# A four-layer mixture-of-experts kernel: the capacity search gets buffers of its own, normalised rows come from ScalarE, and layer 3's gate and up run as two float32r passes

## The chip, the cores and the metric

The kernel runs on one core of a Trainium2 chip. The metric is the device time of one execution in microseconds (us), the median of several runs. Lower is better. The engines are named as the profile names them: PE (TensorE matmuls), PEld (its weight loads), DVE (VectorE), ACT (ScalarE), POOL (GpSimd) and SP (SyncE, which issues most DMAs).

## What is computed

An input of 16 sequences of 256 tokens with 128 features (4096 tokens) goes through four layers. Each layer normalises its input and adds two branches to it:

```python
xn = layernorm(x)
x = x + attn_l(xn) + ffn_l(xn)
```

- Layer 0: attention with 16 heads of 8 features and rotary angles; a mixture of 8 experts (128 to 512 to 128, ReLU), two per token. Each expert keeps at most 1280 tokens, those with the largest gates: a gate under its expert's 1280th largest becomes zero.
- Layer 1: a linear recurrence over each sequence with two projections and a normalisation; 15 experts (128 to 128 to 128), three per token, and one shared expert.
- Layer 2: attention without a bias; 8 experts (128 to 512 to 128), one per token.
- Layer 3: causal attention with a position-dependent bias and an output projection; a dense gated branch, whose weights are integers from -127 to 127, scaled by 1/127:

```python
gate, up = xn @ wg.T, xn @ wu.T        # 128 to 384, wg = w_gate / 127
ffn = (silu(gate) * up) @ wd.T         # 384 to 128
```

## The kernel before

**Tiles.** Tokens stand on the 128 partitions. A block is 512 tokens, so there are 8 blocks; `xb[i]` holds a block of x in SBUF throughout. Routed experts work on groups of blocks: two groups of 4 blocks in layers 0 and 2, four groups of 2 blocks in layer 1 (`GRP`, line 34).

**Order.** Every engine runs its instructions in the order in which they are written, and that order is not written by hand. The code records every operation (class `Engine`, line 312; all of them carry line 350 in the profile), and `Plan.order` (line 186) makes a list for each engine from assumed costs, dependences, free buffers and a due time for each stage and group (`WANTED`, lines 37 to 59). `COLD` (line 35) scales the assumed PE cost. Two score operations on different 32-row strips of the array may be woven together, so that they run at once.

**Buffers.** A tile belongs to a ring, named by its tag, with so many buffers. Within one stream of work (the second argument of `plan.run`) tiles of a ring are taken in turn: as long as a task that has begun still has tiles of the ring to take, no other task of the stream takes one.

**The steps that matter here.**

- `normalize` (line 552): statistics and an inverse root for each token on DVE (`moments`, `inverse_root`), then four DVE operations per block that make `xn`. Four PE transposes and an ACT copy give `xT`. This is done 32 times, for 8 blocks in 4 layers.
- `route_0` (line 1090): router logits of a group, softmax and top two. The gates go to `g0`, which holds all 4096 tokens, expert by expert.
- `sort` (line 1214): gives every choice a place in a table of rows ordered by expert. It takes a tile `m` from the ring `cap` (three buffers) and, in `ranks` (line 673), one from the ring `rank` (one buffer). It ends with indirect DMAs on POOL (line 710), 32 for a group in layer 0, that scatter the rows of `xn`.
- `capacity` (line 627): finds the 1280th largest gate of each expert, bit by bit. Each of 30 steps compares all gates with a candidate (`cap_cmp`), counts (`part_b`), sums over the partitions by a small matmul (`tot_b`) and keeps or drops the bit (`hit`, `cap_thr`). It takes tiles of `cap` and `rank` as well, and it runs in the stream `sort`, emitted after the two sorts of layer 0. Only the combination of layer 0 needs its result.
- `some_tiles` and `slots` (lines 1274 and 727): for every 128 sorted rows an expert's weights are fetched (ring `we`, four buffers) and two matmuls done (`ph`, `po`). The results are gathered by indirect DMA on POOL and added to x in `combine` (line 775).
- Attention: `queries_keys` (line 815) makes queries and keys (`pq`), splits each into a rounded part and a remainder (`half`; in layer 0 with two POOL additions `rope` and `half`), and spreads and fetches them through DRAM (`qm`, `km`, `qx`, `kx`). `front` takes the row maxima of the scores on DVE (`mraw`), `back` the exponentials on ACT (`e`) and the value products (`av`).
- `ffn_3` (line 1325): gate and up are float32 matmuls on `xT` (`pp`, 128 by 512), then tanh on ACT, two DVE products and the down matmul (`po`). `weights_3` (line 1312) loads the three integer matrices as one tile and scales them.

Of the kernel before, what the change touches and what calls it, by code (L numbers as in the profile page):

```python
# [28 lines left out]
BT = 4  # L29
# [4 lines left out]
GRP = {0: 4, 1: 2, 2: 4, 3: 2}  # L34
COLD = 1.2
# [3 lines left out]
    "": (62.9, 0.0, 0.0, 0.0),  # L39
    "att0": (-17.7, 39.8, 36.9, 120.1),  # L40
    "att2": (-125.2, 4.9, -67.1, 45.9),
    "att3": (-85.1, 46.0, 51.1, 102.8),
    "bias2": (-56.2, 153.4, 126.8, 401.9),
    "f3": (166.9, 61.0, 85.4, -51.3),
    "ffn0": (-34.4, 0.0, 32.5, 0.0),
    "ffn1": (2.9, 54.3, 149.0, 145.3),
    "ffn2": (-212.1, 0.0, -158.9, 0.0),
    "kept": (-12.8, 0.0, 0.0, 0.0),
    "rec": (31.1, 105.4, 174.5, 249.2),
    "route0": (-57.1, 0.0, -13.2, 0.0),  # L50
    "route1": (-194.8, -8.3, -27.9, 172.0),
    "route2": (-57.3, 0.0, 43.4, 0.0),
    "sort0": (238.4, 0.0, 310.5, 0.0),
    "sort1": (-45.0, 52.9, 68.6, 170.5),
    "sort2": (-13.5, 0.0, -51.0, 0.0),
    "sum0": (-25.8, 151.2, -71.0, 129.0),
    "sum1": (99.1, 130.3, 136.1, 252.2),
    "sum2": (51.9, 205.8, 84.3, 182.0),
# [28 lines left out]
class Plan:  # L87
# [98 lines left out]
    def order(self):  # L186
# [40 lines left out]
        def room(o):  # L227

            new = [self.ring_of[x] + (x,) for x in o.tiles if x not in placed]
            for g, turn, task, _, x in new:  # L230
                mine = [y for h, _, _, _, y in new if h is g]
                held = task is not None and (x not in turn[: len(mine)] if task["begun"] else bool(turn))
                if held or len(g["free"]) < len(mine):
                    return g, 0.0, new
            at = [sorted(g["free"])[sum(h is g for h, *_ in new) - 1][0] for g, *_ in new]
            return None, max(at, default=0.0), new
# [18 lines left out]
        while True:  # L255
# [17 lines left out]
            take(o, new, t)  # L273
            cost, pair = o.cost, None
            if o.strips:
                for item in sorted(now[e]):
                    p = item[1]
                    if p.strips and not any(x in o.strips for x in p.strips):
                        short, at, new = room(p)
                        if short is None and at <= t:  # L280
                            now[e].remove(item)
                            heapq.heapify(now[e])
                            take(p, new, t)
                            both = [(x.cost - x.rest, x.rest) for x in (o, p)]
                            cost, pair = max(x for x, _ in both) + max(sum(x for _, x in both) - 0.24 * COLD, 0.0), p
                            break
            if e == "PE" and quartered != bool(o.strips):
                cost, quartered = cost + 0.15 * COLD, bool(o.strips)
# [23 lines left out]
class Engine:  # L312
# [5 lines left out]
    def __getattr__(self, method):  # L318
        real = getattr(self.real, method)

        def call(*args, **kw):
# [8 lines left out]
            if self.name == "PE":  # L330
# [6 lines left out]
                else:  # L337
                    cost = max(size(args[2]), T) / 4800
                    strip = args[1].offset // args[1].ap[0][0]
# [12 lines left out]
        return call  # L352

# [57 lines left out]
def four_layers(ctx: ExitStack, tc: tile.TileContext, a: dict, out: bass.AP, at: dict, found=None):  # L411
# [140 lines left out]
    def normalize(srcs, dst_of, name):  # L552

        mv, rs = moments(srcs, name)
        for i, src in enumerate(srcs):
            dst = dst_of(i)
            for t in range(BT):
                k = i * BT + t
                V.tensor_scalar(
                    dst[:, t, :], src[:, t, :], mv[:, k, 0:1], rs[:, k : k + 1], ALU.subtract, ALU.mult  # L560
                )
# [65 lines left out]
    def capacity(g):  # L627
# [37 lines left out]
        run, _ = ranks(cmp, E0, NT, "cap")  # L665
# [7 lines left out]
    def ranks(m, ne, n, name):  # L673
# [11 lines left out]
        run = work.tile([P, ne, n], F32, tag="rank", bufs=1, name=f"rank_{name}")  # L685
# [255 lines left out]
    def back(l, b):  # L941
# [68 lines left out]
        y = work.tile([P, 2, P], F32, tag="y", name=f"y_{nm}")  # L1010
# [39 lines left out]
    g0 = const.tile([P, E0, NT], F32, tag="g0", name="g0")  # L1050
# [14 lines left out]
    for l, (ne, nk, _) in SORTED.items():  # L1065
        tiles[l] = (GRP[l] * BLK * nk - ne) // P + ne
        for g in range(NBLK // GRP[l]):
            shape = [tiles[l] * P, P]
            results[l, g] = dram.tile(shape, F32, tag=f"result{l}{g}", bufs=1, name=f"result{l}{g}")
            tables.setdefault(g * GRP[l], []).append((l, g))  # L1070


    for i, of_ in tables.items():
        n = max(tiles[l] for l, _ in of_)
        table = dram.tile([n * P, P], F32, tag=f"rows{i}", bufs=1, name=f"rows{i}")
        first = tiles[of_[0][0]]
# [3 lines left out]
        for l, g in of_:  # L1080
            rows[l, g] = table[0 : tiles[l] * P, :]

    def choices(l, g):
        ne, nk, _ = SORTED[l]
        n = GRP[l] * BT
        chosen[l, g] = [
            small.tile([P, n, ne], BF16, tag=f"hot{l}{k}", bufs=NBLK // GRP[l], name=f"hot{l}{k}_{g}") for k in range(nk)
        ]

    def route_0(g):  # L1090
        n = GRP[0] * BT
        lgs = work.tile([P, n, E0], F32, tag="lg0", bufs=NBLK // GRP[0], name=f"lgs0_{g}")
        for j in range(GRP[0]):
            i = g * GRP[0] + j
# [8 lines left out]
        gates[0, g] = g0[:, :, g * n : (g + 1) * n].rearrange("p e t -> p t e")  # L1103
# [21 lines left out]

    def new_group(l, g):
        ne, _, _ = SORTED[l]
        n = GRP[l] * BT
        gates[l, g] = small.tile([P, n, ne], F32, tag=f"gates{l}", bufs=NBLK // GRP[l], name=f"gates{l}_{g}")
        choices(l, g)  # L1130

    def route_later(l, g, w, bias):

        ne, nk, _ = SORTED[l]
        n = GRP[l] * BT
        new_group(l, g)
        lgs = small.tile([P, n, ne], F32, tag=f"lgs{l}", bufs=2, name=f"lgs{l}_{g}")
        for k in range(GRP[l]):
            i = g * GRP[l] + k
# [373 lines left out]
```

## Time and profile before

| | |
|---|---|
| time, median of 3 runs (lowest to highest) | 1553.54 us (1546.35 to 1575.81) |
| time of the profiled execution | 1562.79 us |
| its span | 1561.0 us |
| mean granted PE clock | 0.903 |
| PE, PEld busy | 1402.0 us (90%), 992.0 us (64%) |
| DVE, ACT, POOL busy | 1030.2 us (66%), 727.8 us (47%), 433.9 us (28%) |
| HBM read, written | 171.84 MB, 93.19 MB |

In the page's slices the span is cut into 40 equal parts of 39 us, and each digit is an engine's busy share in tenths; PEclk is the granted PE clock in tenths of full speed. A group of instructions is given as operation, output and inputs, shape and count, then busy time and mean duration (ns), then the idle time of the engine just before them and what ended it. A wait is given as the waiting instruction and what released it, with its total, its count and its longest case.

### The profile page before, as it was taken

What the parts mean: (1) busy time and instruction counts of PE and PEld (TensorE: products, weight loads), DVE (VectorE), ACT (ScalarE), POOL (GpSimd) and SP (SyncE); (2) the same over time, 40 slices, a digit from 0 to 9 for tenths busy, and PEclk for the clock granted to TensorE, in tenths of its full rate; (3) what the DMA queues carried; (4) which work ended last, traced back from release to release, by engine and by line L of the source; (5) the groups of instructions that cost most, each with busy time, mean ns of one, the idle gap of its engine ahead of it and who ended that gap; (6) DMA issues with size and microseconds to landing.
All of it is one profiled execution on the core that took longest, in us unless ns stands there. A gap on an engine that the chain in (4) does not pass through costs nothing. (4 is left out here: it accounts for less than half of the span.)

```text
span 1561.0 us, 35056 instructions
## 1 busy us (share of the span) xinstructions
PE 1402.0 (90%) x12870; PEld 992.0 (64%) x12870; DVE 1030.2 (66%) x2796; ACT 727.8 (47%) x1656; POOL 433.9 (28%) x442
## 2 busy tenths in 40 slices
PE   5568879999999899977999999999999999999997
PEld 3345446777878667755565677557687655566665
DVE  8697995444497889688887644877533846765542
ACT  1103555565533566533566676533555335534324
POOL 1201177400444465567135001350301200100000
PEclk9556899999999989988898999889999978999989
DMA  9702366878877767687565686442585313421310
GB/s 298 227 28 81 106 202 221 267 238 274 276 236 232 212 185 202 186 248 241 175 194 175 212 270 200 139 129 76 191 273 171 102 40 110 129 96 49 106 44 8
DMA packets 229517, 267.35 MB, mean 171 GB/s; under 512 B 19657, under 2 KB 188130, under 8 KB 229346
## 3 DMA queue, kind: packets, MB, share of 16 engines
q1 hardware_dynamic: 217058, 239.92, 48.8%
q0 software_dynamic: 12288, 25.19, 5.4%
q8 instruction: 102, 1.67, 0.4%
q14 instruction: 69, 0.57, 0.1%
HBM read 171.84 MB, written 93.19 MB: 170 GB/s over the span
## 5 line engine op out<-in xcount | busy, mean ns | idle before, releaser
L350 DVE TENSOR_REDUCE mraw<-s 128x4 f32<-128x1024 f32 (+2 forms) x512 | 442.4, 884 | 336.1 <-PE s L350 335.1
L350 ACT ACTIVATE e<-s 128x512 f32<-128x512 f32 (+1 forms) x768 | 378.7, 569 | 233.6 <-PE s L350 227.9
L350 POOL DMA_INDIRECT yg<-result,back_l x192 | 184.0, 959 | 466.8 <-DVE x L350 222.5
L350 PE MATMUL s<-kx,qx 32*128 32x256 f32 (+1 forms) x1536 | 207.1, 348 | 64.0 <-DVE mraw L350 60.7
L710 POOL DMA_INDIRECT rows<-xn,back_l x192 | 192.3, 1002 | 186.8 <-DVE past_l L350 85.4
L350 PEld LDWEIGHTS s<-kx,qx 32*128 32x128 f32 x1536 | 128.3, 201 | 167.5 <-DVE mraw L350 90.9
L350 PE MATMUL av<-e,vaug 128*32 128x256 f32 (+1 forms) x3072 | 213.6, 406 | 0.0
L350 PE MATMUL ph<-xg,we 128*128 128x128 f32 x1296 | 187.9, 288 | 8.2 <-DMA we<-in_experts 7.5
L350 PEld LDWEIGHTS ph<-xg,we 128*128 128x128 f32 x1296 | 164.9, 197 | 38.6 <-issue 15.9
L350 PE MATMUL po<-we,h 128*128 128x128 f32 x1296 | 170.9, 279 | 0.3 <-ACT h L350 0.3
L350 PEld LDWEIGHTS po<-we,h 128*128 128x128 f32 x1296 | 157.0, 193 | 11.0 <-issue 4.8
L350 PE MATMUL s<-qx,kx 32*128 32x256 f32 (+1 forms) x1536 | 156.8, 333 | 5.4 <-DVE half L350 1.9
L350 PEld LDWEIGHTS av<-e,vaug 128*32 128x32 f32 x3072 | 88.3, 118 | 83.7 <-issue 44.0
L350 PEld LDWEIGHTS s<-qx,kx 32*128 32x128 f32 x1536 | 103.2, 199 | 56.7 <-issue 31.1
L350 ACT ACTIVATE h<-ph,we 128x128 f32<-128x128 f32 x336 | 97.7, 373 | 74.4 <-PE ph L350 64.6
L350 PE MATMUL s<-top,shift 32*128 32x512 f32 (+2 forms) x1024 | 129.0, 355 | 0.2
L350 DVE SCALAR_TENSOR_TENSOR x<-yg,gate,x 128x128 f32<-128x128 f32 x192 | 63.7, 342 | 37.1 <-DMA yg<-result,back_l 36.2
L350 PE MATMUL pq<-xT,attn 128*128 128x512 f32 x128 | 84.4, 750 | 2.4 <-DMA attn<-in_attn 1.9
L350 PEld LDWEIGHTS s<-top,shift 32*128 32x128 f32 x1024 | 79.0, 203 | 0.7 <-ACT top L350 0.7
L350 ACT COPY ys<-po 128x256 f32<-128x256 f32 (+2 forms) x104 | 45.9, 450 | 66.2 <-PE po L350 54.7
L350 POOL TENSOR_TENSOR rope<-rope,rope 128x512 f32<-128x512 f32 x16 | 20.4, 1276 | 180.9 <-DVE rope L350 158.1
L350 ACT ACTIVATE h<-ph 128x512 f32<-128x512 f32 x78 | 46.8, 599 | 49.7 <-PE ph L350 49.3
(194 smaller groups left out, 1721.9 us busy)
## 6 DMA issues: line engine op xcount, KB each, us to landing
we<-in_experts SPq DMA_DIRECT2D x78, 512.0 KB
qm<-half SPq DMA_DIRECT2D x48, 512.0 KB
qx<-qm SPq DMA_DIRECT2D x96, 256.0 KB
km<-half SPq DMA_DIRECT2D x48, 512.0 KB
kx<-km SPq DMA_DIRECT2D x96, 256.0 KB
we<-in_experts SPq DMA_DIRECT2D x46, 514.0 KB
we<-in_experts SPq DMA_DIRECT2D x152, 128.5 KB
xs<-rows SPq DMA_DIRECT2D x36, 256.0 KB
```

The lines of the kernel that those rows point to most:

```text
L350: self.plan.add(self.name, lambda: real(*args, **kw), [out], ins, cost, sent, strip=strip)
L710: x = nc.gpsimd.indirect_dma_start(out=rows[:, :], out_offset=bass.IndirectOffsetOnAxis(ap=at_, axis=0), in_=src, in_offset=None, bounds_c ...
```

## The change

- The tiles of `capacity` come from the ring `cap` alone, its rank included. `sort` takes `m` from a ring of its own with one buffer, and `rank` is left to the sorts. The search runs in a stream of its own, `kept`.
- `g0` holds the gates token by token; the search reads it through a flipped view.
- `normalize` makes `xn` on ACT, as scale times x plus offset. The offset, minus mean times inverse root, is one more small DVE operation for each block.
- In layer 3, gate and up are float32r matmuls, two for each product: one with a rounded copy of `xT` (ACT) and one with the remainder (POOL). The integer weights are exact as they are, so the factors of 1/127 move into the tanh and the last addition. Gate and up weights are loaded through a buffer of the ring `we`, the down weights apart, and the loading is a stage of its own, `w3`.
- The attention output `y` has one buffer in place of two.
- The planner: groups are given as lists (`GROUPS`) of the same sizes, `COLD` is 1.08 in place of 1.2, all due times are new, and the choice of a partner for a woven pair checks the buffers of both before it takes any. A float32r matmul on all 128 rows has a cost and no strip.

```diff
-GRP = {0: 4, 1: 2, 2: 4, 3: 2}
-COLD = 1.2
+GROUPS = {0: (4, 4), 1: (2, 2, 2, 2), 2: (4, 4), 3: (2, 2, 2, 2)}
+COLD = 1.08
 WANTED = {
-    "": (62.9, 0.0, 0.0, 0.0),
+    "": (1.0, 0.0, 0.0, 0.0),
...
-    "ffn0": (-34.4, 0.0, 32.5, 0.0),
-    "ffn1": (2.9, 54.3, 149.0, 145.3),
-    "ffn2": (-212.1, 0.0, -158.9, 0.0),
-    "kept": (-12.8, 0.0, 0.0, 0.0),
+    "ffn0": (-167.3, 0.0, 3.4, 0.0),
+    "ffn1": (-129.3, 15.5, 33.0, 17.2),
+    "ffn2": (-26.7, 0.0, 24.5, 0.0),
+    "kept": (-193.3, 0.0, 0.0, 0.0),
...
-    "sort0": (238.4, 0.0, 310.5, 0.0),
+    "sort0": (-81.3, 0.0, 115.8, 0.0),
...
+    "w3": (377.1, 0.0, 0.0, 0.0),
 }
...
     def normalize(srcs, dst_of, name):
         mv, rs = moments(srcs, name)
+        off = small.tile([P, len(srcs) * BT], F32, tag="off", bufs=2, name=f"off_{name}")
+        V.scalar_tensor_tensor(off, mv[:, :, 0], -1.0, rs, ALU.mult, ALU.mult)
...
-                V.tensor_scalar(
-                    dst[:, t, :], src[:, t, :], mv[:, k, 0:1], rs[:, k : k + 1], ALU.subtract, ALU.mult
-                )
+                S.activation(dst[:, t, :], src[:, t, :], AF.Identity, bias=off[:, k : k + 1], scale=rs[:, k : k + 1])
...
-        run, _ = ranks(cmp, E0, NT, "cap")
+        run, _ = ranks(cmp, E0, NT, "cap", "cap")
...
-    def ranks(m, ne, n, name):
+    def ranks(m, ne, n, name, tag="rank"):
...
-        run = work.tile([P, ne, n], F32, tag="rank", bufs=1, name=f"rank_{name}")
+        run = work.tile([P, ne, n], F32, tag=tag, bufs=3 if tag == "cap" else 1, name=f"rank_{name}")
...
-        y = work.tile([P, 2, P], F32, tag="y", name=f"y_{nm}")
+        y = work.tile([P, 2, P], F32, tag="y", bufs=1, name=f"y_{nm}")
...
-    g0 = const.tile([P, E0, NT], F32, tag="g0", name="g0")
+    g0 = const.tile([P, NT, E0], F32, tag="g0", name="g0")
...
-        m = work.tile([P, ne, n], F32, tag="cap", bufs=3, name=f"m_{nm}")
+        m = work.tile([P, ne, n], F32, tag="m", bufs=1, name=f"m_{nm}")
...
     def weights_3():
-        w3[0] = wts.tile([P, 3, HID], F32, tag="attn_0", name="w3")
-        raw = w3[0].bitcast(I32)
-        SP.dma_start(raw.rearrange("p k h -> p (k h)"), a["ffn_3"])
-        V.tensor_scalar(w3[0], raw, float(np.float32(1.0 / 127.0)), None, ALU.mult)
+        raw = expert_weights("w3_raw")[:, : 2 * HID].bitcast(I32)
+        SP.dma_start(raw, a["ffn_3"][:, : 2 * HID])
+        w3[0] = wts.tile([P, 2, HID], F32R, tag="attn_0", name="w3")
+        V.tensor_copy(w3[0].rearrange("p k h -> p (k h)"), raw)
+        w3[1] = wts.tile([P, HID], F32, tag="down", name="w3_down")
+        SP.dma_start(w3[1].bitcast(I32), a["ffn_3"][:, 2 * HID :])
+        V.tensor_copy(w3[1], w3[1].bitcast(I32))
+        yield
...
     def ffn_3(i):
+        both = work.tile([P, 2, BLK], F32R, tag="we", bufs=4, name=f"x3_{i}")
+        hi, lo = both[:, 0, :], both[:, 1, :]
+        S.copy(hi, xT[3, i])
+        G.tensor_tensor(lo, xT[3, i], hi.bitcast(F32), ALU.subtract)
+        yield
...
-            PE.matmul(pg, w3[0][:, 0, s], xT[3, i], start=True, stop=True)
-            PE.matmul(pu, w3[0][:, 1, s], xT[3, i], start=True, stop=True)
+            for k, to in enumerate((pg, pu)):
+                PE.matmul(to, w3[0][:, k, s], hi, start=True, stop=False)
+                PE.matmul(to, w3[0][:, k, s], lo, start=False, stop=True)
...
-            S.activation(t, pg, AF.Tanh, scale=0.5)
+            S.activation(t, pg, AF.Tanh, scale=0.5 / 127.0)
...
-        V.scalar_tensor_tensor(xf, po, 0.5, xf, ALU.mult, ALU.add)
+        V.scalar_tensor_tensor(xf, po, 0.5 / 127.0**3, xf, ALU.mult, ALU.add)
...
-    plan.run(kept(), "sort", "kept")
+    plan.run(kept(), "kept", "kept")
...
         if l == 3 and not w3:
-            weights_3()
+            plan.run(weights_3(), "w3", "w3")
```

## The prediction

> **What bounds the kernel now.** I read the page's engine rows and forty slices first, then the busy time by window, then single tiles, groups by shape and the waits.
>
> ```profile
> span 1561.0 us, 35056 instructions
> ...
> PE 1402.0 (90%) x12870; PEld 992.0 (64%) x12870; DVE 1030.2 (66%) x2796; ACT 727.8 (47%) x1656; POOL 433.9 (28%) x442
> ...
> PE   5568879999999899977999999999999999999997
> ...
> PEclk9556899999999989988898999889999978999989
> ```
>
> TensorE is the bound: 90% busy, and in nearly every slice after the fourth at 9. What is lost lies in the first slices, where PE is half busy at half clock, and in a dip near slices 17 and 18. By window (PE, PEld, DVE, ACT, POOL busy, granted clock, DMA share, GB/s):
>
> ```profile
> 0.00:50.00 50.00, 23.16 (x92) 17.40 (x92) 41.08 (x239) 6.30 (x11) 7.02 (x16) 0.89 1.01 292
> 50.00:100.00 50.00, 33.64 (x112) 21.37 (x111) 33.87 (x91) 4.83 (x9) 9.34 (x10) 0.50 0.38 140
> 100.00:150.00 50.00, 37.81 (x232) 23.89 (x231) 37.76 (x99) 12.28 (x25) 2.71 (x3) 0.52 0.12 43
> 150.00:200.00 50.00, 44.00 (x422) 23.81 (x421) 45.96 (x96) 26.70 (x53) 9.04 (x7) 0.90 0.35 121
> ```
>
> Busy times clock is 20.6 + 16.8 + 19.7 + 39.6 = 97 us of full-clock work in the first 200: 103 us are lost. Why nothing fills them, by tile (first and last start):
>
> ```profile
> L350 DVE TENSOR_TENSOR cap_cmp<-g,cand x30: 424/424/427, 69.2 to 159.2; 128x256 f32<-128x256 f32 x30
> ...
> L350 DVE CAST m_l<-hot x8: 267/316/364, 173.1 to 1090.1; 128x128 f32<-128x128 bf16 x4, 128x120 f32<-128x120 bf16 x4
> ...
> L350 PE MATMUL ph<-xg,we x1296: 272/275/583, 257.6 to 1196.4; 128*128 128x128 f32 x186
> ```
>
> The capacity search runs from 69 to 159 us. The first sort starts only at 173, the first expert matmul at 257.6. Until then PE has attention alone, whose scores wait for a DVE that also runs the search: PE is fed by a serial chain. Later, DVE is a second, smaller limit:
>
> ```profile
> PE s L350 <- DVE mraw L350: 60.7, 74, 3.6
> ...
> PE trx L350 <- DVE xn L350: 19.4, 5, 11.3
> ...
> L350 PE MATMUL pp<-xT,w 128*128 128x512 f32 x96 | 45.3, 598 | 0.0
> ...
> L350 DVE TENSOR_SCALAR xn<-x,mv,ny 128x128 f32<-128x128 f32 x128 | 36.0, 343 | 0.7
> ...
> L350 ACT ACTIVATE v<-pb,lam 128x512 f32<-128x512 f32 x8 | 6.2, 778 | 3.3 <-PE pb L350 3.2
> ```
>
> **The Trainium skill.** "TensorE: Matmul & The Clock Gate", Part 1, says the array runs at half clock until some 3.4 us of sustained work; the 0.50 and 0.52 above agree, and so an idle PE is paid twice. The same page, *Back-to-back issue gap*, has N/2.4 + 2.5 ns a pass, 216 ns for 512 columns. The trace agrees where it can: two 512-wide float32r score corrections start 0.21 us apart (164.66 and 164.87). No run here shows a 128-row one. "ScalarE: Activation LUTs", *What ACT_TABLE_LOAD costs*: 186 ns + 0.833 per element, 93 ns more for each pointer operand. With two pointers and 512 columns that is 799; the row above has 778.
>
> **Yardstick.** I price each PE instruction of the two built orders at full clock, as the chain of waits shows it late in the run:
>
> ```profile
> 1188.62 1.79 PE ph L350 x16
> ...
> 1519.97 1.72 PE pp L350 x4
> ```
>
> A float32 matmul is two instructions: 0.224 us for 128 columns, 0.86 for 512; a score of 256 columns about 0.05 (two strips at once), a value product 0.11. The old order sums to 1096 us of work, the new one to 1076. This says where in the work a thing stands, not when.
>
> **Part 1, search and sorts.** The old order has the search at 19 to 52 us of work and the first expert matmul at 112. In the new one the sort of layer 0's first half follows its router, 32 scatters follow on POOL, the experts begin at 17, and the search stands at 38 to 100, mixed with experts and attention. Removed: the empty start. Added: a wait of PE, in order, for the scatters.
>
> When does the new search end? Group 0's gates are written at 32.6 us in the trace; values on ScalarE make this some 4 us later (ACT holds xT of block 1 behind eight new activations). The sort is about 28 DVE operations, 7 us and two PE round trips: first scatter about 46. Scatters follow every 1.28 us (start to start in the trace); 32 of them and one rope addition end about 88. The keys' second rope step is queued behind them on POOL, then their spread and fetch: first scores about 102, where the trace has 80. Router blocks 6 and 7 stand behind these on PE, so the search starts about 120, not 69. PE stands nearly idle from about 55 to 93; that price is in here. Each of the 30 steps then carries 2.1 us of PE work and 76/30 = 2.5 us of DVE work (durations by the groups). The old step took (159.2 - 69.2)/29 = 3.1 us. I take 2.75, between 2.5 and 3.1: end at 120 + 82 = 202 (195 to 213). There PE has done 100. The old kernel has done 52 at 159 and 112 at 257.6, so 100 at about 238. Gain **36 us** (25 to 43). What is late next is PE itself.
>
> The gates now lie token by token, so the compare reads them with a stride. A strided pick of 128 cost 373 ns against 281 in line: +0.18 us for 256, 30 times, 5.5 us of DVE inside the steps, within the 2.5 to 3.1.
>
> **Part 2, gate and up.** 48 float32 matmuls x 0.86 = 41.3 us become 96 passes x 0.216 = 20.7: 20.6 at full clock. The windows from 1100 on average a clock of 0.94, so **-22 us**, all on PE, where PE is 92 to 98% busy. If a 128-row pass costs twice that, nothing is gained (0 to -22); I take the page's price. Added: eight ACT copies (0.63 each), eight POOL subtractions (1.29 each, POOL nearly idle there), hidden since this branch needs only the normalised rows; uncovered, some 2 us per block. The split takes a slot of the expert weights' four; by then those are read in two bursts only. The weights' load moves into the start, 576 KB ahead of the first spread: 2 us at 290 GB/s, ahead of nothing before 46.
>
> **Part 3, normalise.** DVE loses 36.0 us and gains 32 x 0.16 = 5.1. ACT gains 128 x 457 ns (778 less 384 columns at 0.836, the slope between its one-pointer rows 373 and 694) = 58 us, to 51% busy. On PE's path only the wait for scores and transposes counts: after the start some 42 us of the first, 8 of the second. A relief of a tenth of DVE's load where it is 80% busy: -5; activations queued behind exponentials that wait for scores: +2. Net **-3** (-10 to +8).
>
> **Part 4, the new order.** The due times are all new. Paired score groups (two on different strips at once) fall from 122 to 107; a pair saves about 0.43: **+6 us**. Expert work of layer 1 is spread later, which may fill the dip; or the second half of layer 2, whose last expert matmul stands at 889 of 1076 (822 of 1096 before), comes late for layer 3. I take 0, bounds ±25. One buffer instead of two for y: its next writer is an attention half later, 0. The last 20 instructions of PE and of DVE are of the same kinds: the tail stays.
>
> **Sum.** The profiled run took 1562.8 us (span 1561.0, 1.8 around it): 1562.8 - 36 - 22 - 3 + 6 = 1508. The median shown is 1553.5, 0.6% less: 1508 x 0.994 = 1499, taken as **1500 us**.
>
> **Rivals.** (a) *One empty start for another*: POOL's scatters hold experts and keys, and the search's DVE steps are no shorter than 3.1 in company: search end about 220, gain 18, and the pass price doubled: 1562.8 - 18 - 3 + 6 = 1548, 1538 by the median; with only one of the two, 1520. For: PE's order has nothing to do between. Against: from 93 us DMA, PE and ACT, all idle before, have work. (b) *The dip fills too*: early sums of layer 0 let layer 1 start sooner, and the spread expert work covers 600 to 740: 30 us more, 1465. For: 49 us of idle and clock lie in 600 to 800 (85.8 x 0.90 + 88.0 x 0.84 = 151 of 200 done). Against: DVE is 0.84 busy there. (c) *Slower*: normalised rows on ScalarE. PE takes transposes in order; a block's four activations stand behind exponentials on ACT, which themselves wait for scores. If each of the 32 normalisations holds PE by 3.5 us more than now, that is +112: 1612; it decides from (1585 - 1500)/32 = 2.7 us each. Against: PE now waits for xn 19.4 us in all. (d) *The sorts do not move*: excluded by the built order.
>
> **Numbers.** A run-to-run difference within 2% (1522 to 1585) is about what this kernel's times can't tell from no change. Main case, 1478 to 1522: 0.50. (b), below 1478: 0.24. (a), 1522 to 1585: 0.19. (c), over 1585: 0.07. So faster 0.74, same 0.19, slower 0.07. The range 1452 to 1540 leaves out about 0.06 below and 0.12 above; part 4's bounds and the doubled pass lie in it.
>
> **What would show it.** First expert matmul near 94 us; search from about 120 to 200; clock above 0.9 from 100 us; gate and up near 0.43 a product (two passes); xn on ACT near 460 ns. Wrong if PE idles past 110, if the search takes over 3.1 a step, if transposes wait for ACT by tens of us, or if a new hole opens ahead of layer 3's second half.

## The result, and the profile after

The changed kernel takes 1545.08 us (median of 20 runs, 1537.32 to 1553.39), the kernel before 1556.82 in the runs beside it. The ratio is 0.9953, with a 95% interval from 0.9932 to 0.9974: 12 us by the medians and 7 by the ratio, where 55 were forecast, and outside the forecast's range. In a second set of runs the changed kernel took 1544.8 us and the kernel before 1563.6; the ratio there is 0.9885 (0.9847 to 0.9924). The medians are of all runs, the ratios only of those within 1.5% of the fastest of their kernel, so the two can differ. It is the kernel before that varies (medians of 1557 to 1564 us in five sets of runs), and the gain lies between 7 and 19 us, which is less than the 2% that the prediction counts as no change.

The page of the changed kernel, profiled in an execution of 1541.2 us: busy time, and the slices of PE and its clock.

```profile
span 1539.4 us, 35191 instructions
...
PE 1375.4 (89%) x12870; PEld 999.6 (65%) x12870; DVE 1014.5 (66%) x2701; ACT 783.4 (51%) x1792; POOL 442.2 (29%) x450
...
PE   5258999998999997988699989999999997999998
...
PEclk9677999999999999889799988699989999989999
```

PE is as busy as before (89% after 90%), with one nearly empty slice at the start where three or four were half empty. New is a 6 in the clock at slice 25 (counted from 0), where PE is at 9. By window (PE, PEld, DVE, ACT, POOL busy, granted clock, DMA share, GB/s):

```profile
0.00:50.00 50.00, 29.61 (x117) 21.56 (x118) 38.81 (x219) 16.57 (x37) 11.88 (x21) 0.93 1.00 293
50.00:100.00 50.00, 7.81 (x39) 6.08 (x38) 4.94 (x27) 6.96 (x15) 33.29 (x36) 0.56 0.64 210
100.00:150.00 50.00, 44.68 (x290) 35.21 (x288) 41.56 (x91) 16.15 (x33) 10.15 (x8) 0.83 0.55 177
150.00:200.00 50.00, 46.03 (x442) 34.72 (x440) 45.07 (x114) 23.26 (x47) 1.26 (x1) 0.93 0.53 163
```

Busy times clock is 27.5 + 4.4 + 37.1 + 42.8 = 112 us of full-clock work in 200 us, where the kernel before had 97. From 50 to 94 us PE waits for the first sorted rows; after that it is fed. The tiles and waits that the prediction read, in the changed kernel (first the tile views, then waits, then groups by shape):

```profile
L364 DVE TENSOR_TENSOR cap_cmp<-g,cand x30: 610/624/1582, 121.4 to 212.5; 128x256 f32<-128x256 f32 x30
...
L364 DVE CAST m_l<-hot x8: 264/360/1321, 35.8 to 1171.9; 128x128 f32<-128x128 bf16 x4, 128x120 f32<-128x120 bf16 x4
...
L364 PE MATMUL ph<-xg,we x1296: 272/275/582, 94.1 to 1282.4; 128*128 128x128 f32 x186
```

```profile
PE trs L364 <- DMA xs<-rows: 44.0, 3, 42.2
PE s L364 <- DVE mraw L364: 42.0, 51, 9.8
PE trx L364 <- ACT xn L364: 15.9, 2, 11.6
```

```profile
L364 ACT ACTIVATE xn<-x,off,ny 128x128 f32<-128x128 f32 x128 | 52.9, 485 | 28.7 <-DVE off L364 26.5 <-DMA yg<-result,back_l 2.1
...
L364 PE MATMUL pp<-x,w 128*128 128x512 f32 x96 | 29.8, 435 | 0.9 <-DVE half L364 0.9
```

The sort starts at 36 us (173 before), the first expert matmul at 94 (257.6 before), the search at 121, all within 1.5 us of the forecast. The search ends at 213, not 202: a step takes (212.5 - 121.4)/29 = 3.14 us, not 2.75.

**An account.** I summed PE's busy time and clock over windows of 10 us. Idle is the time in which PE isn't busy, loss is busy time times (1 - clock), work is busy time times clock; the three make the span.

| profile | span | idle | loss | work | work by 250 us | after 250: idle, loss, work |
|---|---|---|---|---|---|---|
| before | 1561.0 | 159 | 123 | 1279 | 134 | 89, 77, 1145 |
| changed, first profile | 1539.4 | 164 | 100 | 1276 | 157 | 90, 81, 1119 |
| changed, second profile | 1549.9 | 170 | 105 | 1275 | 157 | 96, 86, 1118 |

By 250 us the changed kernel is 23 us of work ahead. After that it should have 1145 - 23 - 21 (the forecast for the gate and up passes) = 1101 us of work left. It has 1118, and idles and loses some 10 us more than before. So the questions are three: does the start's lead reach the end, what are parts 2 and 3 worth, and what took the 17 + 10 us back?

### The profile page after: what moved, and what is told of

Same layout as the page of the kernel before. It is cut to its first block, busy times and chain, and to the rows that moved or that the text cites. A ratio compares the mean times of both kernels' runs of the same rounds, so it can differ in the third digit from the quotient of the medians.

```text
span 1539.4 us, 35191 instructions
## 1 busy us (share of the span) xinstructions
PE 1375.4 (89%) x12870; PEld 999.6 (65%) x12870; DVE 1014.5 (66%) x2701; ACT 783.4 (51%) x1792; POOL 442.2 (29%) x450
## 4 chain that ended last, share of the span: by engine, by line
PE 38%; DVE 9%; DMA 2%; issue 1%; ACT 1%; POOL 0%; SPq 0%; DVEq 0%; ACTq 0%; POOLq 0%
PE s L364 17%; PE av L364 5%; PE po L364 5%; PE ph L364 4%; DVE mraw L364 3%; DMA yg<-result,back_l 2%; PE pq L364 1%; PE trs L364 1%; PE pp L364 1%; DVE x L364 1%; PE pv L364 1%; PE po1s L364 0%; PE pb L364 0%; PE tra L364 0%; DVE nt L364 0%
## 5 line engine op out<-in xcount | busy, mean ns | idle before, releaser
L364 PE MATMUL av<-e,vaug 128*32 128x256 f32 (+1 forms) x3072 | 204.4, 388 | 1.8 <-ACT e L364 1.4
L364 PE MATMUL ph<-xg,we 128*128 128x128 f32 x1296 | 194.7, 297 | 4.1 <-ACT h L364 1.1
L364 PEld LDWEIGHTS ph<-xg,we 128*128 128x128 f32 x1296 | 171.6, 206 | 28.7 <-issue 9.9
L364 PE MATMUL s<-qx,kx 32*128 32x256 f32 (+1 forms) x1536 | 169.7, 330 | 4.7 <-ACT e L364 1.5
L364 PEld LDWEIGHTS s<-qx,kx 32*128 32x128 f32 x1536 | 112.2, 195 | 56.9 <-issue 25.4
L364 PE MATMUL s<-top,shift 32*128 32x512 f32 (+2 forms) x1024 | 139.4, 350 | 0.1
L364 PE MATMUL trs<-ident,xs 128*128 128x128 f32 x276 | 53.8, 303 | 47.2 <-DMA xs<-rows 44.0
L364 PEld LDWEIGHTS s<-top,shift 32*128 32x128 f32 x1024 | 85.8, 198 | 0.3 <-ACT top L364 0.2
L364 ACT COPY ys<-po 128x256 f32<-128x256 f32 (+1 forms) x104 | 46.0, 447 | 76.5 <-PE po L364 64.0
L364 PE MATMUL pq<-xT,attn 128*128 128x512 f32 x128 | 76.1, 684 | 1.7 <-ACT xT L364 1.7
```

What stands on the lines that cost most here:

```text
L364: self.plan.add(self.name, lambda: real(*args, **kw), [out], ins, cost, sent, strip=strip)
```

## Experiments

In most of these kernels the order of every engine is the planner's order for the changed kernel, and only what is issued differs, so that a difference is that of the edit and not of a new order. The diffs leave out the test that keeps the original operation while the order is made. Times are medians, compared with the changed kernel's 1545 us, and by ratio with the kernel before that ran beside them. Each experiment left one profile.

**e1 and its control.** First the changed kernel again (c0).

> The changed kernel as it is, for a second profile beside the experiments. If the half clock at 972 to 1003 us of the first profile belongs to the order of the work, it comes again within 10 us of that place, and the search again takes 3.1 us a step; if it is chance, the half-clock stretches after 250 us lie elsewhere in the second profile, though their sum stays near 185 us. Time: 1545 us, 0.995 of before.

1544.8 us. (The times of these half-clock stretches count from 11 us before the span's start; the windows put the stretch named here at 961 to 992.) It came again at the same place in both profiles. Windows of the second:

```profile
960.00:970.00 10.00, 9.81 (x71) 6.49 (x71) 7.48 (x24) 4.40 (x11) 7.22 (x9) 0.56 0.30 85
970.00:980.00 10.00, 10.00 (x70) 6.41 (x68) 6.44 (x19) 3.98 (x9) 0.85 (x1) 0.50 0.37 113
980.00:990.00 10.00, 10.00 (x70) 6.02 (x68) 2.04 (x4) 2.62 (x6) 0.00 (x0) 0.50 0.17 52
```

PE is busy almost without a gap, and has half the clock for 30 us and more. What runs there, in the timeline of the first profile, are single score groups:

```profile
979.01 0.69 PE L364 MATMUL s<-qx,kx 32*128 32x256 f32 x4
979.50 0.63 PE L364 MATMUL s<-top,shift 32*128 32x256 f32 x4
980.06 0.61 PE L364 MATMUL s<-laterT,ident 128*128 128x256 bf16 x2
```

Two of the three kinds work on 32 of the array's 128 rows; the third, about a third of the time, on all of them. The stretch belongs to the order, not to chance.

Then **the gates expert by expert** (e1), with the two views of them changed to match.

```diff
-    g0 = const.tile([P, NT, E0], F32, tag="g0", name="g0")
+    g0 = const.tile([P, E0, NT], F32, tag="g0", name="g0")
```

> The changed kernel, every engine in the same order, with the gates laid out expert by expert again, so that the compare of the search reads them in line. Theory S (the steps of the prediction have the right places but wrong sizes: a search step is DVE's own time, and what is gained at the start stays): the compare falls from 0.66 to 0.42 us, the step from 3.14 to 2.9, the search ends 7 us sooner, and the run is 5 to 8 us shorter than the changed kernel. Rival L (a later stage takes back what the start gains): the search ends 7 us sooner, the run stays within 2 us. Rival P (PE's round trip paces the step, not DVE): the step stays at 3.1 us.

1541.5 us, ratio 0.9876 (0.9827 to 0.9926).

```profile
L364 DVE TENSOR_TENSOR cap_cmp<-g,cand x30: 424/426/1437, 122.0 to 208.7; 128x256 f32<-128x256 f32 x30
```

A compare is 0.20 us shorter, a step 0.15 (2.99), the search ends 4 us sooner and the run 3 us: the direction of S at about half of its size, and the intervals of the two kernels overlap. What the strided gates cost the search is shown, 4 us; that they cost the run as much is likely by e12 and e13 below.

**Parts 3 and 2 taken back, one at a time.** Rows on DVE (e2), in ACT's place in the order:

```diff
-                S.activation(dst[:, t, :], src[:, t, :], AF.Identity, bias=off[:, k : k + 1], scale=rs[:, k : k + 1])
+                V.tensor_scalar(dst[:, t, :], src[:, t, :], rs[:, k : k + 1], off[:, k : k + 1], ALU.mult, ALU.add)
```

> The changed kernel in the same order, but the 128 operations that make the normalised rows run on DVE, where ACT has them in the order. Theory S (part 3 is worth little): DVE has 44 us more, ACT 53 less; 2 to 8 us slower than the changed kernel, mostly from longer waits of PE for the row maxima. Rival A (ACT's place for it costs what DVE wins): no change within 2 us, or up to 8 us faster with shorter waits of PE for transposed rows.

1556.2 us, 11.4 more, above S's band. It is not by longer waits: the wait for row maxima is 43.8 us where the changed kernel's two profiles have 42.0 and 48.7, and idle time did not grow (165). The loss to half clock is 113 us where those two have 100 and 105.

One float32 matmul for the two passes (e3):

```diff
-                PE.matmul(to, w3[0][:, k, s], hi, start=True, stop=False)
-                PE.matmul(to, w3[0][:, k, s], lo, start=False, stop=True)
+                PE.matmul(to, w3[0][:, k, s].bitcast(F32), hi.bitcast(F32), start=True, stop=True)
```

> The changed kernel in the same order, but each gate and up product is one float32 matmul with the rounded copy of the rows; the product with the remainder is left out, and the two operations that make copy and remainder stay. Theory S: the 48 products take about 45 us of PE where the 96 passes took 30, and the run is 14 to 20 us slower than the changed kernel, since PE is the bound there. Rival L (that stage has slack of its own): under 6 us slower.

1551.4 us, 6.6 more, in neither band. The account says how: work is 1296 us, 21 more than in the changed kernel; idle is 162 (5 less than the mean of 164 and 170), loss 93 (9 less than that of 100 and 105). 21 - 5 - 9 = 7. By this account two thirds of the work that part 2 takes off PE comes back as waiting and as half clock. (By the tile `pp` alone, busy time times clock is 45.5 us here and 28.1 in the changed kernel, 17 apart; the other 4 are within what the work of profiles in one order differs by, 1275 to 1280 us.)

**Four runs on a chip that stood still** (c1, e4, e5, e6): the kernel before, and the kernels of e7, e12 and e13 below.

> The kernel before as it is, for a second profile. If the profile that the prediction worked from is a fair one, full-clock work, idle time and loss to the half clock of PE come out within 10 us of its 1277, 159 and 125 us, and the half clock from 1279 to 1306 us comes again.

> The changed kernel in its own order with parts 2 and 3 taken back at once: normalised rows on DVE, one float32 matmul with the rounded copy for each gate and up product (the product with the remainder is left out). What stays of the change is the search's buffers, the gates by token and the order. Theory S, that parts 2 and 3 are worth 6.6 and 11.4 us as the single runs measured and simply add: 1545 + 18 = 1563 us, so that the new order and the earlier sorts gain nothing on the kernel before (1557 to 1564). Rival N (the two share one loss, the half clock): 1552 to 1557.

> The changed kernel in the same order with every compare of the search done twice: 30 x 0.66 = 20 us more on DVE between 120 and 212 us. Theory S (what the start gains or loses stays to the end): the search ends near 232 us, the run is 12 to 20 us longer. Rival L (a later stage takes it back): search ends near 232, the run under 5 us longer.

> The changed kernel in the same order with the gates expert by expert, and with only a quarter of the columns (64 of 256) compared and counted in each step, so that the threshold comes from a quarter of the tokens: a step has 0.8 us less DVE work than the changed kernel's. Theory S: DVE paces the step, which falls from 3.14 to about 2.4 us; search ends near 192 us; the run is 12 to 20 us shorter (1525 to 1533). Rival P (PE's work of 2.1 us and the round trips in each step take over): step 2.8 or more, search ends after 202, run 3 to 8 us shorter. Rival L: search ends sooner, run within 3 us of the 1541.5 with flat gates.

The kernel before took 1796 us here, and the four 1793, 1764, 1796 and 1759. Every engine stood idle for long stretches that no recorded event ends. Waits in the first of these profiles:

```profile
DVE mraw L350 <- remote: 127.4, 16, 13.7
...
PE s L350 <- issue: 56.5, 39, 10.7
```

In the first profile of the kernel before no such wait of these two tiles is listed. These times decide nothing; the last three were run again elsewhere. No second profile settles whether the first one of before was fair; but its clock over the whole span, 0.903, is that of the kernel's other runs (means of 0.904 to 0.907 in four sets of 27 to 62).

**Parts 2 and 3 taken back together** (e7: the edits of e2 and e3).

> The kernel of e4 once more, since that run fell on a chip where all engines stood idle for no recorded reason in long stretches, and its kernel before took 1796 us. Normalised rows on DVE, one float32 matmul with the rounded copy for each gate and up product (the product with the remainder is left out), the changed kernel's order. If parts 2 and 3 add: 1545 + 6.6 + 11.4 = 1563 us. If they share one loss: 1552 to 1557.

1559.9 us, ratio to the kernel before 0.9989 (0.9954 to 1.0025): 15 us more than the changed kernel, near the 18 of the two single runs. What is left of the change (the buffers, the earlier sorts, the new order, and small things such as the copies and the weights' loads of part 2) gains nothing measurable by itself. Yet by 250 us this kernel has done 166 us of work, 31 more than the kernel before. After 250 us it has 1133 us of work, 93 idle and 80 of loss, 1306 in all. The kernel before, had it been 31 us ahead, would have needed 1311 - 31 = 1280. So some 26 us are lost again after 250, which I put down to the new order, and most is PE time: 1133 where 1145 - 31 = 1114 were due. By tile, the scores carry it: their busy time times clock is 457 to 462 us in five profiles of the new order, and 438 in the kernel before.

**One pass** (e8).

```diff
-                PE.matmul(to, w3[0][:, k, s], hi, start=True, stop=False)
-                PE.matmul(to, w3[0][:, k, s], lo, start=False, stop=True)
+                PE.matmul(to, w3[0][:, k, s], hi, start=True, stop=True)
```

> The changed kernel in the same order, but gate and up are one float32r pass with the rounded copy; the pass with the remainder is left out. PE has 48 x 0.216 = 10.4 us less to do. Theory W (PE's work in that stage is time, as the prediction had it): 9 to 10 us shorter than the 1545 of the changed kernel. Theory C (the clock is granted by how much of the array has worked, so that work taken out comes back as half clock and idle time, as the 20.7 us of work between one float32 matmul and two passes gave only 6.6 us): 2 to 5 us shorter, with more half-clock time after 600 us.

1550.0 us, between 1528.7 and 1574.7 in 22 runs, ratio 0.9957 (0.9925 to 0.9989). W's 9 to 10 us would be a ratio of 0.982 to 0.989, so W does not show; C's 2 to 5 us (0.985 to 0.994) are at the edge of the interval. The profiled run, with a span of 1530.5 and a loss of 92 us, is the second fastest of the 22 and does not stand for them. What does is the mean clock that is on record for every run:

| gate and up | runs | mean clock over the span |
|---|---|---|
| one float32 matmul (e3) | 15 | 0.919 |
| two float32r passes (the changed kernel) | 29 | 0.912 |
| one float32r pass (e8) | 22 | 0.904 |

The less PE has to do in that stage, the lower the clock that it gets: C's direction. In the traces the clock is either whole or half, so at 0.904, 0.096 x 2 x 1550 = 298 us are at half clock; at 0.912, 0.088 x 2 x 1545 = 272. The same record explains the spread: in 62 runs of the kernel before, beside e7 to e10, the shortest (1540 us) had 0.918 and the longest (1598) 0.878. And e2 belongs here: its 22 runs average 0.906.

**Part 3 alone, in the old order** (e9).

```diff
-                V.tensor_scalar(
-                    dst[:, t, :], src[:, t, :], mv[:, k, 0:1], rs[:, k : k + 1], ALU.subtract, ALU.mult
-                )
+                S.activation(dst[:, t, :], src[:, t, :], AF.Identity, bias=mv[:, k, 0:1], scale=rs[:, k : k + 1])
```

(One more DVE operation a block first writes the offset over the mean in `mv`.)

> The kernel before in its own order, with only part 3: the 128 operations that make the normalised rows on ACT. If part 3 is worth what its removal from the changed kernel cost (11.4 us), the kernel before gets 8 to 14 us faster (ratio 0.991 to 0.995). If ACT's place suits only the changed order (rival O), no change or slower: ratio 0.998 to 1.006. The prediction's own figure, -3 us, is a ratio of 0.998.

1575.8 us, ratio 1.0062 (1.0019 to 1.0106): some 10 us slower by the ratio. DVE has 31 us less to do, and PE's wait for row maxima falls from 60.7 to 57.4 us, but PE is idle 8 us more in the profile (of a run 25 us longer than this kernel's shortest). The mean clock of its 20 runs is 0.900, that of the kernel before beside it 0.906. Taking the edit out of one order costs 11 us, putting it into the other some 10: rival O. Both kernels put the rows into the place that the order had made for another engine. What was measured may be the price of leaving the plan, rather than the worth of part 3; a kernel planned anew for either engine was not run.

**The first sort due later** (e10, with the flat gates of e1).

```diff
-    "sort0": (-81.3, 0.0, 115.8, 0.0),
+    "sort0": (-60, 0.0, 115.8, 0.0),
```

> The changed kernel with the gates expert by expert, and the due time of layer 0's first sort moved from -81.3 to -60, which makes a new order: the first scores stand ahead of the first expert matmul on PE, the last operation of block 0's keys stands behind 21 scatters on POOL in place of 32, and the search stands at 29 to 90 of 1076 us of PE's work in place of 39 to 100. Theory S (the empty stretch from 55 to 94 us can be filled, and what the start gains stays): the first scores start near 85 us, PE idles 10 us less there, and the run is 3 to 10 us shorter than the 1541.5 with flat gates alone. Rival R (the rest of the order, which moves too, decides): 1542 to 1560 in spite of an earlier start.

1581.5 us, ratio 1.015 (1.0107 to 1.0193). The first score starts at 82.7 us, but PE idles only 3.5 us less between 50 and 100, and by 250 us the work is 167, 10 more than in the changed kernel and 3 more than with flat gates alone. What follows undoes it: rival R, and by more than R's band. One window of this kernel:

```profile
1050.00:1200.00 150.00, 128.00 (x1035) 81.07 (x1035) 75.27 (x185) 43.44 (x100) 19.06 (x20) 0.68 0.26 86
```

The same window of the changed kernel:

```profile
1050.00:1200.00 150.00, 145.70 (x1512) 104.64 (x1512) 105.46 (x244) 76.92 (x174) 39.85 (x41) 0.95 0.46 145
```

One due time of one stage at the start moved the rest so that this window alone does 51 us less work (128.0 x 0.68 = 87 against 145.7 x 0.95 = 138).

**Half of the pairs unwoven** (e11).

```diff
+            turn += m is not None
+            if m is not None and turn % 2:
+                for call in self.ops[n].calls + self.ops[m].calls:
+                    call()
+                continue
```

> The changed kernel in the same order, but every second of its 107 woven pairs of score groups (54 of them) is issued one group after the other. The prediction's price, 0.43 us a pair, gives 54 x 0.43 = 23 us more. If the 19 us that the scores take more in the changed kernel (458 us of full-clock work against 438) come from the 15 pairs that the new order lost, a pair is worth 1.3 us: 54 x 1.3 = 70 us more, and still more by half clock.

1576.5 us, but of four runs three took 1576 to 1581 and one 1546, as long as the changed kernel; with so few, the price of a pair in time stays open. By the three it is 0.6 us, near the prediction's 0.43 and far from 1.3; by the one it is nothing. The profile is of one of the three. There the scores' work grows by 6 us only (464) for 54 pairs, so 15 lost pairs would explain some 2 of the 19 us; what else makes the scores dearer in the new order stays open. The loss grows from 100 or 105 to 131. The page's clock row of this profile:

```profile
PEclk9578999999998998978899887899999998859987
```

In this profile a pair is worth its clock more than its work: two groups at once use 64 rows, one uses 32.

**The search longer (e12) and shorter (e13).**

```diff
             V.tensor_tensor(cmp, g, over(cand.bitcast(F32)), ALU.is_ge)
+            V.tensor_tensor(cmp, g, over(cand.bitcast(F32)), ALU.is_ge)
```

> The kernel of e5 once more, on another chip: every compare of the search done twice, same order. The search ends near 233 us in place of 212. Theory S (the start's time stays to the end): 12 to 20 us longer than the changed kernel's 1545. Rival L (a stage from 300 to 500 us that waits for DVE takes it up): under 6 us longer.

1568.7 us, ratio 1.0072 (1.0044 to 1.0101).

```profile
L364 DVE TENSOR_TENSOR cap_cmp<-g,cand x30: 610/624/1573, 122.5 to 232.0; 128x256 f32<-128x256 f32 x30
L686 DVE TENSOR_TENSOR cap_cmp<-g,cand x30: 609/620/671, 123.1 to 232.6; 128x256 f32<-128x256 f32 x30
```

```diff
-                V.tensor_tensor(cmp, g, over(cand.bitcast(F32)), ALU.is_ge)
-                tot = total(cmp, f"b{bit}")
+                few = slice(0, 8)
+                V.tensor_tensor(cmp[:, :, few], g[:, :, few], over(cand.bitcast(F32))[:, :, few], ALU.is_ge)
+                tot = total(cmp[:, :, few], f"b{bit}")
```

> The kernel of e6 once more, on another chip: gates expert by expert and a quarter of the columns compared and counted in each step, so that the threshold comes from a quarter of the tokens. A step takes 2.8 us, the search ends near 205. Theory S: 6 to 9 us shorter than the changed kernel (1536 to 1539). Rival L: within 3 us of the 1541.5 with flat gates.

1532.7 us, ratio 0.9841 (0.9790 to 0.9892).

```profile
L364 DVE TENSOR_TENSOR cap_cmp<-g,cand x30: 198/225/228, 121.4 to 195.8; 128x64 f32<-128x64 f32 x30
```

A search that ends 20 us later makes the run 24 longer, one that ends 17 sooner makes it 12 shorter, and 4 sooner made 3: **the start's time reaches the end**, at 0.7 to 1.2 for one. Rival L falls. And a step is mostly DVE's own time: 0.62 us more of it makes the step 0.64 longer (3.78), 0.63 less (0.43 in the compare, 0.20 in the count) makes it 0.57 shorter (2.57).

**What PE's clock counts** (e14). Behind the last work of the changed kernel stand 1500 matmuls, in fifteen stretches of a hundred, whole-array ones between the others:

```diff
+    for rows_, cols_ in (full, (32, P), full, (64, P), full, (96, P), full, (P, 32), full, (P, 64), full, (48, P), full, (40, P), full):
+        for _ in range(100):
+            nc.tensor.matmul(to[:cols_, :], wide[:rows_, :cols_], wide[:rows_, :BLK], start=True, stop=True)
```

> The changed kernel with 1400 float32r matmuls of 512 columns behind its last work, a hundred of each kind one after the other: on the whole array, on 32 rows, whole, 64 rows, whole, 96 rows, whole, 32 columns, whole, 64 columns, whole, 48 rows, whole, 40 rows, whole. PE is never idle in them. Theory C (the clock of a window follows how much of the array worked in the one before, full from about 0.38 of its rows times columns): a few us after each change half clock for 32 rows, 32 columns and 40 rows (0.25, 0.25, 0.31), full for 64 and 96 rows, 64 columns and the whole (0.5 and more), and for 48 rows (0.375) either. Rival B (only idle time takes the clock away): full clock in all of them.

Windows inside the seven kinds (32, 64, 96 rows; 32, 64 columns; 48, 40 rows), of these matmuls alone (PE busy, PEld busy, clock):

```profile
1560.00:1598.00 38.00, 38.00 (x99) 28.86 (x98) 0.56 0.00 0
1628.00:1646.00 18.00, 18.00 (x81) 14.59 (x80) 1.00 0.00 0
1674.00:1692.00 18.00, 18.00 (x82) 14.89 (x81) 1.00 0.00 1
1719.00:1738.00 19.00, 19.00 (x83) 8.93 (x82) 1.00 0.00 1
1765.00:1784.00 19.00, 19.00 (x85) 11.05 (x84) 1.00 0.00 0
1812.00:1845.00 33.00, 33.00 (x82) 25.29 (x81) 0.52 0.00 0
1875.00:1909.00 34.00, 34.00 (x81) 26.11 (x81) 0.50 0.00 0
```

PE has no gap in any of them. With 32, 40 or 48 rows it has half the clock, from some 4 us after the rows change (hence 0.56 and 0.52) for as long as that lasts; with 64 rows or more it has all of it. Rival B falls, and so does C's size for columns: 32 columns on all rows keep the full clock. Rows count, columns don't, and for work of one kind the bound lies between 48 and 64 of 128 rows. Two strips woven, and mixtures of narrow and whole groups like the one at 961 us, were not tested by themselves.

**16-bit hits** (e15).

```diff
-            V.tensor_tensor(cmp, g, over(cand.bitcast(F32)), ALU.is_ge)
-            tot = total(cmp, f"b{bit}")
+            V.tensor_tensor(few, g, over(cand.bitcast(F32)), ALU.is_ge)
+            tot = total(few, f"b{bit}")
```

> The changed kernel in the same order with the gates expert by expert, and the zeros and ones that each compare of the search writes as bf16, which the count then reads (the counts stay exact). With flat gates alone the compare took 0.42 us and the count 0.42. If DVE is quicker with 16-bit data in either, by 0.1 us or more, a step is some 0.1 shorter, the search ends 3 us sooner and, since the start's time reaches the end, the run takes 1536 to 1539. If not, 1541 as with flat gates alone.

1541.2 us, ratio 0.9914 (0.9888 to 0.9940): as with flat gates alone.

```profile
L364 DVE TENSOR_REDUCE part_b<-cap_cmp x30: 419/420/423, 122.4 to 206.9; 128x8 f32<-128x256 bf16 x30
```

The count takes 0.42 us from bf16 as it did from float32. Flat gates, with or without this, are the fastest exact version that was run: 3 to 4 us under the changed kernel, in two sets of runs.

**The buffers taken back** (e16).

```diff
-        m = work.tile([P, ne, n], F32, tag="m", bufs=1, name=f"m_{nm}")
+        m = work.tile([P, ne, n], F32, tag="cap", bufs=3, name=f"m_{nm}")
...
-        run, _ = ranks(cmp, E0, NT, "cap", "cap")
+        run, _ = ranks(cmp, E0, NT, "cap")
...
-    plan.run(kept(), "kept", "kept")
+    plan.run(kept(), "sort", "kept")
```

> The changed kernel with part 1's buffers taken back: the sorts' tile comes from the ring of the search again, the search's ranks from the sorts' one buffer, and the search runs in the sorts' stream. All due times stay, the order is made anew: on PE the search stands at 18 to 34 of 1076 us of work (39 to 100 in the changed kernel), the first expert matmul at 69 (18). Theory S: the start is that of the kernel before or worse: search from about 70 to 160 us, first expert matmul after 230, work done by 250 us near 130, and the run 20 to 35 us longer than the changed kernel: 1565 to 1580. Rival R (the later order decides, as in the run with the sort due later): anything from 1540 to 1600, not in line with the work done by 250 us.

1660.0 us, ratio 1.0714 (1.0678 to 1.0750). Two tiles of this kernel:

```profile
L364 DVE TENSOR_TENSOR cap_cmp<-g,cand x30: 609/611/622, 65.4 to 144.2; 128x256 f32<-128x256 f32 x30
...
L364 PE MATMUL ph<-xg,we x1296: 272/275/583, 210.8 to 1408.0; 128*128 128x128 f32 x186
```

Without the buffers the start is the old one again: search first, experts from 211, 121 us of work by 250, 36 less than in the changed kernel. The other 79 us of the 115 are lost later, in an order that these due times were not made for. Both theories hold in part: S for the start, R for the rest, though the run is longer than either had it.

## Why the prediction was wrong

Its sum was -36 - 22 - 3 + 6 = -55. From the runs the terms are -23 (part 1, by work), -6.6 (part 2), -11.4 (part 3, with the doubt above), and what is left to the 7 to 19 us measured is part 4: +22 to +34. That last term is a remainder, not a measurement.

**Part 1: the place right, the size not.** "First scatter about 46" came at 44.3, their end, "about 88", at 86.4; first expert matmul and start of the search are within 1.5 us. The failed term is "I take 2.75, between 2.5 and 3.1". It measured 3.14, so that the search ended at 213, and the gain, by work at 250 us, is 23, not 36. Two things were left out of 2.75. The compare grew by 0.23 us, not 0.18 (657 ns against 424, by the means). And the clock between 100 and 150 us was 0.83, where "above 0.9 from 100 us" was expected; three of the first eight steps take 4.4 to 4.8 us. The time itself was not absorbed: e12 and e13 show that it reaches the end.

**Part 2: work is not time.** The price of the work was nearly right: 17 us by the tile, 21 by all of PE, for 20.6 at full clock (a pass, priced at 0.216 us, took 0.23 in e14). The failed step is "-22 us, all on PE, where PE is 92 to 98% busy". Taken back, it was worth 6.6. In e3 9 us of the 21 came back as loss and 5 as idle time. A PE that is 95% busy can be busy at half clock, and an attention chain need not start sooner because other matmuls end sooner. The clock falls step by step as matmuls on all 128 rows are taken out (0.919, 0.912, 0.904 over all runs of e3, the changed kernel and e8), which fits e14, where only work on 64 rows or more kept it. That these matmuls hold the clock up for the narrow scores beside them is argued from the two; no run separates it from a mere change of timing.

**Part 3: the reason wrong, the worth not known.** The forecast was -3, by shorter waits (its failed step: "only the wait for scores and transposes counts"). Its removal costs 11.4 us, hardly any of it by those waits, and with a lower clock, 0.906 for 0.912. In the old order the same edit costs some 10, with a lower clock too. So the sign is owed to the order in which it was tried, and the worth of the part by itself was not measured. Rival (c), transposes that wait for ACT, did not come: 15.9 us in all.

**Part 4: the step that decides.** "+6", 15 pairs at 0.43 us, was neither borne out nor refuted by e11. The failed step is "I take 0, bounds ±25" for the rest of the new order: a term put at nothing, without a cause for either sign, that came out at +16 to +28, in the upper part of its bounds or past them. In e7, where little but the start and the order differs from the kernel before, a lead of 31 us is lost whole. Some 19 us of it are in the scores' own PE time, of which lost pairs explain some 2; the cause of the rest stays open. That a new order alone can swing the time so far is shown by e10: one due time, 40 us against flat gates alone. In e16, where the buffers differ as well, 79 us are lost far from the stage that was touched. The prediction read the order in us of PE work, and such a list has no clock in it.

Of its marks of failure one came true, "if the search takes over 3.1 a step". The result lies in the band of rival (a), 1522 to 1585, which had 0.19; its mechanism was half right, since the step was 3.1 but no pass price doubled: a pass at full clock starts 0.23 us after the one before (e14). Its own sum with the step alone, 1520, misses by 25 us, so that the time fell into its band is in part luck. Rival (b), the dip, did not come: between 600 and 800 us the changed kernel does 145 us of work by the windows, the kernel before 151.

## What to carry over

Where an order is planned by list, price an edit by its stage and then ask what the order of everything else becomes: here the rest took back as much as the best part had gained. Keeping the order and changing one operation tells what the operation is worth in that order; the same edit can gain in one and lose in another, and part of either may be the price of leaving the plan. And count PE's time with its clock: in e14, work on 48 rows of the array or fewer ran at half clock however dense it was, so two narrow groups side by side may be worth more than the time that they share.

## What the runs showed of the hardware

The Trainium skill, "TensorE: Matmul & The Clock Gate", Part 1, says the clock follows how busy PE has recently been, and its section *HAM oscillation — how this bites in real kernels* warns of idle gaps over some 3.4 us. The traces agree for gaps (clock 0.56 between 50 and 100 us, where PE waits until 94), but busy is not enough: 100 matmuls without a gap on 32, 40 or 48 rows got half of it (0.56, 0.50 and 0.52 in windows of which the first and the last hold a few us before the change), those on 64 and 96 rows, and on all rows with 32 or 64 columns, got 1.00. So the 0.50 and 0.52 between 50 and 150 us of the kernel before, which the prediction put down to an idle PE, may be owed to narrow scores as well: PE was busy for 71 of those 100 us. At half clock the matmuls of 512 columns start 0.43 us apart, on the whole array at full clock 0.23. The times of one kernel go with its clock from run to run (1540 us at 0.918, 1598 at 0.878). DVE counts 256 bf16 values no faster than 256 float32 ones (420 ns both), and a compare that reads its float32 operand at a stride of 32 bytes takes 624 ns (median) where it takes 424 in line.
